# Diffusion steps with a PSUM operand in every VectorE instruction, and an init without GpSimd

## The chip, the cores and the metric

One core of a Trainium2 chip runs the whole program. Its engines are TensorE (PE; its weight loads are listed as PEld), VectorE (DVE), ScalarE (ACT), GpSimd (POOL) and SyncE (SP), which issues the DMAs. The metric is the device time in microseconds; the time before is the median of three runs.

## The reference

Four layers follow each other on an image of 48 x 48 pixels with 768 channels, all in fp32: attention with an MLP, a Fourier layer, a diffusion scan, and another Fourier layer. The change concerns the third:

```python
B_proj = silu(x @ W_B + b_B + B_bias).reshape(Bb, Hh, Ww, N, R)      # N = 64, R = 4
C_proj = silu(x @ W_C + b_C + C_bias).reshape(Bb, Hh, Ww, N, R)
Xb = silu(x @ W_X + b_X); alpha = sigmoid(x @ W_dec + b_dec)
theta = x @ W_th + b_th;  gamma = sigmoid(x @ W_lam + b_lam)
for i in range(NITERS):                                             # 12
    inj = _rope(B_base, theta * (i + 1)) * Xb
    Hst = diffuse(Hst)              # depthwise 3x3 convolution + conv_b
    if prev is None:
        Hst = alpha * Hst + inj
    else:
        Hst = alpha * Hst + (1.0 - gamma) * alpha * prev + gamma * inj
    prev = inj
Hg = _rope(C_base, theta * NITERS) * Hst
return silu(Ho @ W_out + b_out)     # Ho is Hg with its axes moved
```

## The kernel before, in words

The program runs attention, projection, MLP, first Fourier layer (`afno_first`), the scan (`scan_phase`) and the second Fourier layer one after the other. A tile framework inserts the semaphores and orders each engine's instructions.

In the scan a partition holds one column position of one of two image rows: rows of a pair sit at partitions 0 to 47 and 64 to 111, and 24 pairs (NPR) lie along the free axis. 256 channels (64 n times 4 r) make 6144 elements per partition.

The init (lines 722 to 835) forms everything that the steps need. Its weights `w` are loaded at line 729, when the scan begins. A loop `q` of six rounds takes four pairs (R4) each. For each pair 12 matmuls (line 758) make two PSUM tiles, `pa` and `pb`, four buffers each, and VectorE adds the bias on the way to `za` and `zb` (lines 759 and 760). ScalarE applies silu and sigmoid, and sine and cosine after a range reduction on VectorE (`reduce_angle`). Then VectorE and GpSimd share the elementwise work: `turn` (lines 793 to 798) rotates with two of its four products on GpSimd; GpSimd also multiplies by x (line 801) and by gamma (lines 820 and 825). The results are the state `H`, two sources `s0` and `s1`, `al` (alpha), `c1` (2 cos theta), and `cr`, which goes to DRAM for the end (line 835).

The source of each iteration follows a recurrence: with s for this iteration and s' for the last, the next is c1 * s - s'. It is written over s'.

The steps (lines 863 to 891) are 11 iterations over 8 groups of 8 channels n. TensorE does the convolution as a product with banded matrices (`bands`, line 872): 32 matmuls a group, 64 records[...]. Row 48 of the bands holds the convolution's bias, and row 48 of H holds ones. Since the init computes on all 128 partitions, it fills the gap rows 48 to 63 with other values; four DMAs (line 858, source `gap`) then set them in H, s0, s1 and c1. `alr` is alpha repeated over r, made by ScalarE (line 859). A group's PSUM tile (one of four, two banks each) is used so:

```python
V.tensor_tensor(y, ps[:, :, :half], alr[:, ch], ALU.mult)     # line 875
V.tensor_tensor(Hd, y, fl(sc), ALU.add)                       # line 878
GP.tensor_tensor(t, sc[:, ch], c1[:, m0 : m0 + GC], ALU.mult) # line 881
e = GP if gr % 8 in (1, 4, 7) else V
e.tensor_tensor(sn[:, ch], t, sn[:, ch], ALU.subtract)        # line 883
```

(shapes shortened). In the last iteration the source is not updated; `cr` is loaded (line 887) and H is multiplied by it into `hg`, six products a group (line 891). Then 24 pairs are transposed and multiplied by the output weights (lines 908 to 920).

Of the kernel before, what the change touches and what calls it, by code (L numbers as in the profile page):

```python
# [18 lines left out]
P = 128  # L19
# [655 lines left out]
def reduce_angle(nc, pool, th, n, name):  # L675

    MAGIC = 1.5 * 2.0**23
    C1 = 6.28125
    C2 = math.floor((2.0 * math.pi - C1) * 2.0**22) / 2.0**22
    C3 = 2.0 * math.pi - C1 - C2  # L680
    k = pool.tile([P, n], F32, tag="sc_k", name=f"{name}_k")
    r = pool.tile([P, n], F32, tag="sc_r", name=f"{name}_r")
    nc.vector.tensor_scalar(k, th, 1.0 / (2.0 * math.pi), MAGIC, ALU.mult, ALU.add)
    nc.vector.tensor_scalar(k, k, MAGIC, None, ALU.subtract)
    nc.vector.scalar_tensor_tensor(out=r, in0=k, scalar=-C1, in1=th, op0=ALU.mult, op1=ALU.add)
    nc.vector.scalar_tensor_tensor(out=r, in0=k, scalar=-C2, in1=r, op0=ALU.mult, op1=ALU.add)
    nc.vector.scalar_tensor_tensor(out=r, in0=k, scalar=-C3, in1=r, op0=ALU.mult, op1=ALU.add)
    PI = 3.1415925
    nc.vector.tensor_scalar(r, r, -PI, PI, ALU.max, ALU.min)
    a = pool.tile([P, n], F32, tag="sc_a", name=f"{name}_a")  # L690
    nc.scalar.activation(a, r, AF.Abs)
    return r, a


def scan_phase(tc, ident, wts, xT, xT_close, cr_d, out_open):
# [11 lines left out]
    (w_d, b0_d, b1_d, cb_d, bands_d, gap_d, wo_d, bo_d) = wts  # L707
    R4 = 4
    NQ = G // 2 // R4
    NPR = G // 2  # L710
    NCR = NN * RR
# [3 lines left out]
    with tc.tile_pool(name="sc_s", bufs=1, side="left") as sp:  # L715
        s0 = sp.tile([P, NN, RR, NPR], F32, tag="s0", name="s0")
        s1 = sp.tile([P, NN, RR, NPR], F32, tag="s1", name="s1")
        with tc.tile_pool(name="sc_state", bufs=1, side="left") as stp:
            H = stp.tile([P, NN, RR, NPR + 2], F32, tag="H", name="H")
            al = stp.tile([P, NN, NPR], F32, tag="al", name="al")  # L720
            c1 = stp.tile([P, NM, NPR], F32, tag="c1", name="c1")
            GP.memset(H, 0.0)
            with (
# [4 lines left out]
                w = wp.tile([P, NC, NA + NB2], F32, tag="w", name="w")  # L728
                nc.sync.dma_start(w, w_d.rearrange("(c p) n -> p c n", p=P))
                bias = load_bcast(nc, wp, b0_d, NA + NB2, "bias")  # L730
                bias1 = load_bcast(nc, tp, b1_d, NA + NB2, "zb")
# [5 lines left out]
                def temp(shape, tag, q, bufs=1):  # L737
                    return tp.tile([P, *shape], F32, tag=tag, name=f"{tag}_{q}", bufs=bufs)

                def sincos(th, q, nm):  # L740
                    r, a = reduce_angle(nc, tp, th, NM * R4, f"{nm}_{q}")
# [3 lines left out]
                    nc.scalar.activation(co.rearrange("p m t -> p (m t)"), a, AF.Sin, bias=halfpi, scale=-1.0)  # L745
                    return co, sn

                for q in range(NQ):
                    prs = slice(q * R4, (q + 1) * R4)
                    za = temp([NA, R4], "za", q)  # L750
                    zb = temp([NB2, R4], "zb", q)
                    for t in range(R4):
# [3 lines left out]
                        for ps, c0, n in ((pa, 0, NA), (pb, NA, NB2)):  # L756
                            for cc in range(NC):
                                nc.tensor.matmul(ps[:, :n], lhsT=xT[:, cc, tok : tok + P], rhs=w[:, cc, c0 : c0 + n], start=cc == 0, stop=cc == NC - 1)
                        V.tensor_tensor(za[:, :, t], pa[:, :NA], bias[:, :NA], ALU.add)
                        V.tensor_tensor(zb[:, :, t], pb[:, :NB2], bias[:, NA:], ALU.add)  # L760
# [7 lines left out]
                    alq = al[:, :, prs]  # L768
# [8 lines left out]
                    c1q = c1[:, :, prs]  # L777
                    V.tensor_scalar(c1q, cs, 2.0, None, ALU.mult)

                    def over_r(v, n):  # L780
                        return v.unsqueeze(2).to_broadcast([P, n, RR, R4])
# [5 lines left out]
                    def turn(out, in_, co, si, nm):  # L787
# [5 lines left out]
                        GP.tensor_tensor(m0, b, si, ALU.mult)  # L793
                        V.tensor_tensor(oa, a, co, ALU.mult)
                        V.tensor_tensor(oa, oa, m0, ALU.subtract)
                        GP.tensor_tensor(m1, b, co, ALU.mult)
# [4 lines left out]
                    GP.tensor_tensor(g.rearrange("p (n r) t -> p n (r t)", r=RR), g.rearrange("p (n r) t -> p n (r t)", r=RR), x.rearrange("p r t -> p (r t)").unsqueeze(1).to_broadcast([P, NN, RR * R4]), ALU.mult)  # L801
                    i03 = H[:, :, :, 1 + q * R4 : 1 + (q + 1) * R4]
# [6 lines left out]
                    V.tensor_tensor(be, alq, om.to_broadcast([P, NN, R4]), ALU.mult)  # L809
                    bc = temp([NN, R4], "bc", q)  # L810
                    gc = temp([NM, R4], "gc", q)
                    V.tensor_tensor(gc, c1q, ga.to_broadcast([P, NM, R4]), ALU.mult)
# [3 lines left out]
                    gab = ga.to_broadcast([P, NCR, R4])  # L816
                    flat = lambda v: v.rearrange("p n r t -> p (n r) t")

                    u = temp([NCR, R4], "u", q)
                    GP.tensor_tensor(u, i0, gab, ALU.mult)  # L820
                    t0 = s0[:, :, :, prs]
                    V.tensor_tensor(t0, g3, over_r(be, NN), ALU.mult)
                    V.tensor_tensor(flat(t0), flat(t0), u, ALU.add)
                    u = temp([NCR, R4], "u", f"{q}_1")
                    GP.tensor_tensor(u, g, gab, ALU.mult)
                    t1 = s1[:, :, :, prs]
# [4 lines left out]
                    V.tensor_tensor(ac, alq, cb.unsqueeze(2).to_broadcast([P, NN, R4]), ALU.mult)  # L831
                    V.tensor_tensor(i03, i03, over_r(ac, NN), ALU.add)
                    cr = temp([NCR, R4], "u", f"{q}_2")
                    turn(cr, c, cs12, sn12, "c")
                    nc.sync.dma_start(cr_d[:, q], cr)
            xT_close()
            K = 112
            GC = 8
            with (
# [11 lines left out]
                for gr in range(NN // GC):  # L851
                    ch = slice(gr * GC, (gr + 1) * GC)
                    nc.sync.dma_start(bands[:K, ch], bands_d[:, ch])
                    if gr == 0:
                        gap = slice(G, HD)
                        for t, n, v in ((c1, NM * NPR, 1), (s1, NCR * NPR, 0), (s0, NCR * NPR, 0), (H, NCR * (NPR + 2), 0)):
                            t = t[gap].rearrange("p n t -> p (n t)") if t is c1 else t[gap].rearrange("p n r t -> p (n r t)")
                            nc.sync.dma_start(t, gap_d[v : v + 1, :n].to_broadcast([HD - G, n]))
                    nc.scalar.copy(alr[:, ch], al[:, ch].unsqueeze(2).to_broadcast([P, GC, RR, NPR]))
                s = [s0, s1]  # L860
                for it in range(1, ITERS):
                    sc, sn = s[it % 2], s[(it + 1) % 2]
                    for gr in range(NN // GC):
                        ch = slice(gr * GC, (gr + 1) * GC)
                        m0 = (gr * GC) % NM
                        nm = f"{it}_{gr}"
                        ps = pss[gr % 4]
                        for k in range(GC):
                            n = gr * GC + k
                            cols = slice(k % 4 * RR * NPR, (k % 4 + 1) * RR * NPR)  # L870
                            for i, (r0, d) in enumerate(((0, 1), (HD, 1), (0, 0), (HD, 2))):
                                nc.tensor.matmul(ps[r0 : r0 + G, k // 4, cols], lhsT=bands[:K, n, i, :], rhs=H[:K, n, :, d : d + NPR], start=i < 2, stop=i >= 2)  # L872
                        half = GC * RR * NPR // 2
                        y = tp.tile([P, GC * RR, NPR], F32, tag="y", name=f"y_{nm}")
                        V.tensor_tensor(y.rearrange("p (b n) t -> p b (n t)", b=2), ps[:, :, :half], alr[:, ch].rearrange("p (b n) r t -> p b (n r t)", b=2), ALU.mult)  # L875
                        fl = lambda v: v[:, ch].rearrange("p n r t -> p (n r) t")
                        Hd = fl(H)[:, :, 1 : 1 + NPR]
                        V.tensor_tensor(Hd, y, fl(sc), ALU.add)  # L878
                        if it + 1 < ITERS:
                            t = tp.tile([P, GC, RR, NPR], F32, tag="t", name=f"t_{nm}")  # L880
                            GP.tensor_tensor(t, sc[:, ch], c1[:, m0 : m0 + GC].unsqueeze(2).to_broadcast([P, GC, RR, NPR]), ALU.mult)  # L881
                            e = GP if gr % 8 in (1, 4, 7) else V
                            e.tensor_tensor(sn[:, ch], t, sn[:, ch], ALU.subtract)  # L883
                        else:

                            cr = tp.tile([P, NQ, GC * RR, R4], F32, tag="cr", name=f"cr_{gr}", bufs=2)
                            nc.sync.dma_start(cr, cr_d[:, :, gr * GC * RR : (gr + 1) * GC * RR])
                            hg = sn.rearrange("p n r t -> p (n r t)").rearrange("p (t n) -> p n t", t=NPR)
                            for q in range(NQ):
                                prs = slice(q * R4, (q + 1) * R4)  # L890
                                V.tensor_tensor(hg[:, gr * GC * RR : (gr + 1) * GC * RR, prs], Hd[:, :, prs], cr[:, q], ALU.mult)
# [3 lines left out]
        with (  # L895
# [8 lines left out]
            for p2 in range(NPR // 2):  # L904
                ps = pt.tile([P, 512], F32, tag="t", name=f"ht_{p2}")
                for t in range(2):
                    for j in range(2):
                        nc.tensor.transpose(ps[:, (2 * t + j) * P : (2 * t + j + 1) * P], hg[:, 2 * p2 + t, j * P : (j + 1) * P], ident)
# [16 lines left out]
def block_kernel(ctx: ExitStack, tc: tile.TileContext, a: dict):  # L925
# [31 lines left out]
    x2T, x2T_close = opened("x2T", [P, NC, G * HD], "right")  # L957
    afno_first(tc, ident, a, xA, x2T)
# [9 lines left out]
    wts = [a[k] for k in ("W_scan", "b_scan", "bias_scan", "conv_b", "bands", "gap", "W_out", "b_out")]  # L968
    cr_d = dram.tile([P, 6, NN * RR, 4], F32, tag="cr_d", name="cr_d")
    x3 = scan_phase(tc, ident, wts, x2T, x2T_close, cr_d, out_open)  # L970
# [80 lines left out]
def shape_constants():  # L1051
# [18 lines left out]
    for h in range(2):  # L1070
# [9 lines left out]
        "gap": f(np.stack([np.full(NN * RR * 26, 1.0), np.full(NN * RR * 26, 2.0)]), 2, NN * RR * 26),  # L1080

# [10 lines left out]
def banded(w, b):  # L1092
# [6 lines left out]
    m = np.zeros((112, NN, 4, G), np.float32)  # L1099
    for i, dhs in enumerate(((1, 2), (None, 0), (0, 1), (2, None))):  # L1100
# [6 lines left out]
        if i < 2:  # L1107
            m[G, :, i, :] = b[:, None]
# [47 lines left out]
```

## Time and profile before

| | us |
|---|---|
| median of three runs (4768.79 to 4771.67) | 4770.26 |
| the profiled execution | 4773.5 |
| its span, first to last instruction | 4771.3 |
| first matmul of the scan's init starts | 3709.63 |
| its last add into H (line 832) starts | 3920.13 |
| first matmul of the steps starts | 3934.50 |
| first product of the steps (line 875) starts | 3952.45 |
| first matmul of the output product starts | 4283.39 |

The starts are on the axis of the profiled execution, counted from its first instruction. The page of the profile gives for each engine its busy time in forty slices, the groups of instructions by source line with mean duration and idle time before them, and the chain of work that ended last. Queries of the trace add the tables of busy time for chosen stretches, the durations of one line, the waits, and instructions in order of time. A busy VectorE instruction may include time in which it stands still: its duration runs from its start to its end, whatever held it up. In the group lines an entry such as `H<-y,s 128x768` names output and inputs with partitions and elements.

### The profile page before, as it was taken

To read this page: it belongs to the slowest core of one execution; us is meant where nothing else is said; L and a number is where in the kernel's file an instruction comes from. 1 tells how busy PE (TensorE), PEld (TensorE's weight loads), DVE (VectorE), ACT (ScalarE), POOL (GpSimd) and SP (SyncE) were. 2 spreads that over 40 slices of the span, in tenths; PEclk is the share of its full clock that TensorE was granted. 3 is DMA by queue.
4 is the path that set the end of the run, shared out by engine and by line. 5 is a ranking of instruction groups with operands and counts; after the bars stand their busy time and mean duration, and the time that the engine had idled before them with its cause. 6 is when DMAs were issued, how large, how long until landed. Compare 5 with 4: busy or idle time off the path is not lost.

```text
span 4771.3 us, 55325 instructions
## 1 busy us (share of the span) xinstructions
PE 4439.8 (93%) x23674; PEld 2736.8 (57%) x23674; DVE 1792.5 (38%) x2434; ACT 1045.8 (22%) x1660; POOL 449.8 (9%) x292
## 2 busy tenths in 40 slices
PE   8999699999999999989999999999998847789998
PEld 5555344444444444555555555556777637776776
DVE  4212155554555555410110100002343679983333
ACT  2111133333333333100110100002222330003221
POOL 0000000000000000110000000000000338630000
PEclk9999899999999999989999999999998978899887
DMA  4132522121212112151111111110000020010001
GB/s 153 40 84 64 127 41 50 30 50 40 50 30 50 30 33 54 43 133 50 50 50 50 50 53 48 49 47 2 3 5 1 31 65 18 2 31 6 18 20 30
DMA packets 144904, 212.46 MB, mean 45 GB/s; under 512 B 24620, under 2 KB 112684, under 8 KB 142236
## 3 DMA queue, kind: packets, MB, share of 16 engines
q1 hardware_dynamic: 144652, 208.85, 16.6%
q8 instruction: 188, 3.08, 0.3%
q14 instruction: 64, 0.52, 0.0%
HBM read 166.74 MB, written 42.07 MB: 44 GB/s over the span
## 4 chain that ended last, share of the span: by engine, by line
PE 82%; DVE 10%; ACT 2%; issue 2%; DMA 1%; SPq 1%; POOL 1%; DVEq 0%; POOLq 0%; ACTq 0%
PE s L342 18%; PE acc L528 12%; PE h L520 11%; PE av L363 9%; PE v L252 3%; DVE H L878 3%; PE pj L482 3%; PE q L167 3%; PE k L241 3%; PE f_f L996 2%; DVE y L875 2%; DVE s L883 2%; PE f_z L631 2%; PE f_z L630 1%; PE f_w L1040 1%
## 5 line engine op out<-in xcount | busy, mean ns | idle before, releaser
L342 PE MATMUL s<-qa,ka 128*128 128x384 f32 x2592 | 896.1, 496 | 41.0 <-DMA qa<-rh_d 40.0
L342 PEld LDWEIGHTS s<-qa,ka 128*128 128x128 f32 x2592 | 475.9, 190 | 457.1 <-issue 170.2
L352 DVE TENSOR_TENSOR acc<-acc,p 128x768 f32<-128x768 f32 x576 | 552.7, 959 | 487.8 <-ACT p L344 487.0
L344 ACT ACTIVATE p<-s 128x768 f32<-128x768 f32 x648 | 525.1, 811 | 820.2 <-PE s L342 820.2
L528 PE MATMUL acc<-w,ht 128*128 128x384 f32 x1728 | 581.6, 487 | 9.9 <-DMA w<-in_mlp_w_dram 9.9
L520 PE MATMUL h<-x2nT,w 128*128 128x384 f32 x1728 | 583.0, 488 | 5.6 <-ACT ln_sd L69 3.5
L528 PEld LDWEIGHTS acc<-w,ht 128*128 128x128 f32 x1728 | 329.3, 191 | 240.2 <-DMA w<-in_mlp_w_dram 10.5
L363 PE MATMUL av<-p,vt 128*64 128x384 f32 x2592 | 465.5, 494 | 0.0
L520 PEld LDWEIGHTS h<-x2nT,w 128*128 128x128 f32 x1728 | 329.3, 191 | 236.0 <-issue 6.3
L533 DVE TENSOR_TENSOR xA<-acc,xA 128x384 f32<-128x384 f32 x36 | 20.1, 557 | 1078.7 <-PE acc L528 1078.4
L872 PE MATMUL c<-H,bands 112*48 112x96 f32 x5632 | 266.8, 260 | 118.4 <-DVE y L875 67.8
L872 PEld LDWEIGHTS c<-H,bands 112*48 112x48 f32 x5632 | 257.8, 132 | 127.6 <-DVE y L875 75.8
L363 PEld LDWEIGHTS av<-p,vt 128*64 128x64 f32 x2592 | 166.9, 136 | 272.1 <-issue 272.1
L522 ACT ACTIVATE ht<-h,ml_b 128x384 f32<-128x384 f32 x144 | 83.6, 580 | 988.5 <-PE h L520 961.8
L477 POOL TENSOR_TENSOR pj_x<-pj_x,pj_b 128x768 f32<-128x768 f32 x18 | 34.3, 1913 | 2029.1 <-DVE acc L352 1874.7
L881 POOL TENSOR_TENSOR t<-s,c 128x768 f32<-128x768 f32 x80 | 168.1, 2106 | 65.0 <-DVE s L883 50.8
L241 PE MATMUL k<-xnT,w 128*128 128x384 f32 x432 | 148.9, 494 | 1.1 <-ACT rw L181 1.1
L252 PE MATMUL v<-w,xnT 128*128 128x384 f32 x432 | 149.0, 495 | 0.0
L878 DVE TENSOR_TENSOR H<-y,s 128x768 f32<-128x768 f32 x88 | 145.1, 1648 | 3.1
L631 PE MATMUL f_z<-f_w,f_o 97*96 97x96 f32 x800 | 142.3, 262 | 1.0 <-POOL f_o L620 1.0
L630 PE MATMUL f_z<-f_w,f_o 97*96 97x96 f32 x800 | 142.7, 262 | 0.0
L167 PE MATMUL q<-xnT,w 128*128 128x384 f32 x432 | 142.2, 488 | 0.0
(185 smaller groups left out, 4350.4 us busy)
## 6 DMA issues: line engine op xcount, KB each, us to landing
w<-in_mlp_w_dram SPq DMA_DIRECT2D x168, 384.0 KB
qa<-q_d SPq DMA_DIRECT2D x72, 288.0 KB
qa<-rw_d SPq DMA_DIRECT2D x72, 216.0 KB
x<-in_x_dram SPq DMA_DIRECT2D x18, 384.0 KB
w<-in_qkv_w_dram SPq DMA_DIRECT2D x18, 384.0 KB
q_d<-qT SPq DMA_DIRECT2D x6, 1152.0 KB
k_d<-kT SPq DMA_DIRECT2D x6, 1152.0 KB
v_d<-v SPq DMA_DIRECT2D x6, 1152.0 KB
```

What stands on the lines that cost most here:

```text
L167: nc.tensor.matmul(ps[:, :TB], lhsT=ws[0][:, cc, pr * P : (pr + 1) * P], rhs=xnT[:, cc, tok], start=cc == 0, stop=cc == NC - 1)
L241: nc.tensor.matmul(ps[:, :TB], lhsT=ws[1][:, cc, pr * P : (pr + 1) * P], rhs=xnT[:, cc, tok], start=cc == 0, stop=cc == NC - 1)
L252: nc.tensor.matmul(ps[:, :TB], lhsT=xnT[:, cc, (3 * blk + t) * P : (3 * blk + t + 1) * P], rhs=ws[2][:, cc, cols], start=cc == 0, stop=cc ...
L342: nc.tensor.matmul(ps[:, s, :QB], lhsT=kas[2 * (pr % 2) + s][:, kt * P : (kt + 1) * P], rhs=chunks[c][s][:, g, :], start=True, stop=True)
L344: nc.scalar.activation(p, ps[:, :, :QB], AF.Exp)
L352: nc.vector.tensor_tensor(probs[c], probs[c], p, ALU.add)
L363: nc.tensor.matmul(avs[c][rows, :QB], lhsT=pairs[pr][:, kt, rows], rhs=p[:, s, :], start=kt == 0, stop=kt == NT - 1)
L520: nc.tensor.matmul(ps[:, :TB], lhsT=w1s[f][:, cc, :], rhs=xnT[:, cc, :], start=cc == 0, stop=cc == NC - 1)
L528: nc.tensor.matmul(acc[t][i][:, :TB], lhsT=ht[:, t * P : (t + 1) * P], rhs=w2t[:, i * TB : (i + 1) * TB], start=k == 0, stop=k == NF - 1)
L631: nc.tensor.matmul(out, lhsT=o1[:, j, 0:2, :].rearrange("c r h -> c (r h)"), rhs=w2t[:, 1, :], start=False, stop=True)
L872: nc.tensor.matmul(ps[r0 : r0 + G, k // 4, cols], lhsT=bands[:K, n, i, :], rhs=H[:K, n, :, d : d + NPR], start=i < 2, stop=i >= 2)
L878: V.tensor_tensor(Hd, y, fl(sc), ALU.add)
```

## The change

Four things are altered in `scan_phase`, its helper and its caller.

The steps: the product with alpha is written back into PSUM, and the sum into H reads it from there. GpSimd still makes t; ScalarE copies t into the same PSUM tile, and VectorE's update reads it from PSUM. All updates are VectorE's. They stand one group later in the program (`after`), also the products with `cr`, of which there are now eight a group.

The ones row: it moves from row 48 to row 112 of H and bands. The init works on partitions 0 to 111 (`K`), so the gap DMAs and their input are removed; GpSimd sets partitions 96 to 127 before the init. Gap rows 48 to 63 keep what the init puts there, as the bands are zero in them.

The init: eight rounds of three pairs. GpSimd's products go to VectorE, except those with gamma, which ScalarE does as multiplications by a scalar per partition, three for each tile. `za` and `u` get two buffers, `cr` its own.

The weights: the caller opens `wsc` and loads it before `afno_first`.

```diff
-    R4 = 4
+    R4 = 3
+    K = 112
...
+            top = slice(96, P)
             GP.memset(H, 0.0)
+            for t, v in ((al, 0.0), (c1, 2.0), (s0, 1.0), (s1, 1.0), (H[:, :, :, 1 : 1 + NPR], 1.0)):
+                GP.memset(t[top], v)
...
-                w = wp.tile([P, NC, NA + NB2], F32, tag="w", name="w")
-                nc.sync.dma_start(w, w_d.rearrange("(c p) n -> p c n", p=P))
...
-                    za = temp([NA, R4], "za", q)
+                    za = temp([NA, R4], "za", q, 2)
...
-                                nc.tensor.matmul(ps[:, :n], lhsT=xT[:, cc, tok : tok + P], rhs=w[:, cc, c0 : c0 + n], start=cc == 0, stop=cc == NC - 1)
+                                nc.tensor.matmul(ps[:K, :n], lhsT=xT[:, cc, tok : tok + K], rhs=w[:, cc, c0 : c0 + n], start=cc == 0, stop=cc == NC - 1)
...
+                    def by_gamma(out, in_):
+                        for t in range(R4):
+                            nc.scalar.mul(out[:, :, t], in_[:, :, t], ga[:, 0, t : t + 1])
...
-                        GP.tensor_tensor(m0, b, si, ALU.mult)
+                        V.tensor_tensor(m0, b, si, ALU.mult)
...
-                        GP.tensor_tensor(m1, b, co, ALU.mult)
+                        V.tensor_tensor(m1, b, co, ALU.mult)
...
-                    GP.tensor_tensor(u, i0, gab, ALU.mult)
+                    by_gamma(u, i0)
...
-                    GP.tensor_tensor(u, g, gab, ALU.mult)
+                    by_gamma(u, g)
...
-                    cr = temp([NCR, R4], "u", f"{q}_2")
+                    cr = temp([NCR, R4], "cr", q)
                     turn(cr, c, cs12, sn12, "c")
-                    nc.sync.dma_start(cr_d[:, q], cr)
+                    nc.sync.dma_start(cr_d[:K, q], cr)
+            w_close()
             xT_close()
-            K = 112
+            K1 = K + 1
...
-                    nc.sync.dma_start(bands[:K, ch], bands_d[:, ch])
-                    if gr == 0:
-                        gap = slice(G, HD)
-                        for t, n, v in ((c1, NM * NPR, 1), (s1, NCR * NPR, 0), (s0, NCR * NPR, 0), (H, NCR * (NPR + 2), 0)):
-                            t = t[gap].rearrange("p n t -> p (n t)") if t is c1 else t[gap].rearrange("p n r t -> p (n r t)")
-                            nc.sync.dma_start(t, gap_d[v : v + 1, :n].to_broadcast([HD - G, n]))
+                    nc.sync.dma_start(bands[:K1, ch], bands_d[:, ch])
...
-                        V.tensor_tensor(y.rearrange("p (b n) t -> p b (n t)", b=2), ps[:, :, :half], alr[:, ch].rearrange("p (b n) r t -> p b (n r t)", b=2), ALU.mult)
...
-                        V.tensor_tensor(Hd, y, fl(sc), ALU.add)
...
-                            e = GP if gr % 8 in (1, 4, 7) else V
-                            e.tensor_tensor(sn[:, ch], t, sn[:, ch], ALU.subtract)
...
+                    pv = ps[:, :, :half]
+                    V.tensor_tensor(pv, pv, banks(alr, gr), ALU.mult)
+                    by_bank = lambda v: v.rearrange("p (b n) r t -> p b (n r) t", b=2)
+                    V.tensor_tensor(by_bank(H[:, ch])[:, :, :, 1 : 1 + NPR], pv.rearrange("p b (n t) -> p b n t", t=NPR), by_bank(sc[:, ch]), ALU.add)
+                    if it + 1 < ITERS:
+                        t = tp.tile([P, GC, RR, NPR], F32, tag="t", name=f"t_{it}_{gr}")
                         m0 = (gr * GC) % NM
...
+                        GP.tensor_tensor(t, sc[:, ch], c1[:, m0 : m0 + GC].unsqueeze(2).to_broadcast([P, GC, RR, NPR]), ALU.mult)
+                        nc.scalar.copy(pv, t.rearrange("p (b n) r t -> p b (n r t)", b=2))
...
+                def after(it, gr):
+
+                    sn = s[(it + 1) % 2]
+                    if it + 1 < ITERS:
+                        sb = banks(sn, gr)
+                        V.tensor_tensor(sb, pss[gr % 4][:, :, :half], sb, ALU.subtract)
+                        return
...
+                    for q in range(NQ):
+                        prs = slice(q * R4, (q + 1) * R4)
+                        V.tensor_tensor(hg[:K, nr, prs], Hd[:K, :, prs], crs[gr][:K, q], ALU.mult)
...
+                for i in range(len(steps) + 1):
+                    if i < len(steps):
+                        step(*steps[i])
+                    if i:
+                        after(*steps[i - 1])
...
     x2T, x2T_close = opened("x2T", [P, NC, G * HD], "right")
+    wsc, wsc_close = opened("wsc", [P, NC, a["W_scan"].shape[1]], "right")
+    nc.sync.dma_start(wsc, a["W_scan"].rearrange("(c p) n -> p c n", p=P))
     afno_first(tc, ident, a, xA, x2T)
...
-            m[G, :, i, :] = b[:, None]
+            m[112, :, i, :] = b[:, None]
```

## The prediction

> **What bounds the kernel now.** I read the busy table by stage first, then the groups of the diffusion steps, the tiles of one step, the waits, and the order of time of one group.
>
> The stages of the scan (stretch, length, busy time of each engine with its instruction count, granted TensorE clock, DMA share, GB/s):
>
> ```profile
> core 0: us, PE busy (x) PEld busy (x) DVE busy (x) ACT busy (x) POOL busy (x), PEclk, DMA share, GB/s
> 3700.00:3709.60 9.60, 0.86 (x6) 0.62 (x4) 1.17 (x3) 0.00 (x0) 5.64 (x1) 0.50 0.67 232
> 3709.60:3883.90 174.30, 157.78 (x576) 113.73 (x576) 128.62 (x205) 59.86 (x84) 57.65 (x34) 0.94 0.04 14
> 3883.90:3934.50 50.60, 0.04 (x1) 0.03 (x1) 36.25 (x54) 17.99 (x25) 20.06 (x10) 0.55 0.52 121
> 3934.50:3952.40 17.90, 13.31 (x256) 13.11 (x256) 11.08 (x5) 0.00 (x0) 17.90 (x10) 0.79 0.53 141
> 3952.40:4231.60 279.20, 216.07 (x4480) 207.73 (x4480) 272.22 (x186) 0.00 (x0) 202.17 (x99) 0.91 0.01 2
> 4231.60:4278.30 46.70, 39.16 (x903) 38.36 (x904) 45.61 (x85) 0.00 (x0) 1.84 (x1) 0.96 0.18 53
> ```
>
> VectorE is busy 272.22 of 279.20 us in the steps: it is the bound there, and ScalarE does nothing. In the 50.60 us before them TensorE stands still.
>
> Three lines on VectorE and GpSimd in the steps (duration min/median/max):
>
> ```profile
> L875 DVE TENSOR_TENSOR y<-c,alr x88: 940/945/955, 3952.4 to 4274.7; 128x768 f32<-128x768 f32 x88
> L878 DVE TENSOR_TENSOR H<-y,s x88: 957/1807/1919, 3953.4 to 4275.8; 128x768 f32<-128x768 f32 x88
> L883 DVE TENSOR_TENSOR s<-t,s x50: 957/2384/2587, 3932.9 to 4232.7; 128x768 f32<-128x768 f32 x50
> L881 POOL TENSOR_TENSOR t<-s,c x80: 1795/1820/2543, 3931.1 to 4227.5; 128x768 f32<-128x768 f32 x80
> ```
>
> All are 768 elements per partition. The one that reads PSUM and SBUF (y) never leaves 0.95 us; those that read SBUF twice need 0.96 us at best and 1.8 to 2.4 us usually. In order of time (start, length) the long ones end with a GpSimd instruction and not with their own work:
>
> ```profile
> 4053.42 0.94 DVE L875 TENSOR_TENSOR y<-c,alr 128x768 f32<-128x768 f32 x1
> 4053.58 1.82 POOL L881 TENSOR_TENSOR t<-s,c 128x768 f32<-128x768 f32 x1 [0.89 <-DVE s L883]
> 4054.40 1.81 DVE L878 TENSOR_TENSOR H<-y,s 128x768 f32<-128x768 f32 x1
> ```
>
> GpSimd ends at 4055.40; H ends 0.81 us later, at 4056.21: it stood still until then. The entry to the steps shows in the waits:
>
> ```profile
> PE pa L758 <- DMA w<-in_W_scan_dram: 8.8, 1, 8.8
> ...
>   DMA H<-in_gap_dram: 50.6, 1
> ```
>
> 8.8 us for the projection weights, and 50.6 us that end with the gap transfer into H, though most of them are VectorE's tail of the init: its last add into H (L832) starts at 3920.13.
>
> **What the Trainium skill says.** "SBUF — State Buffer", Who interferes with whom: VectorE with two SBUF inputs and a GpSimd instruction that reads SBUF exclude each other, and with at most one SBUF input they don't; a VectorE instruction in a 2-port mode is also excluded. The trace agrees: 0.945 us against 1.807, and the tensor_scalar of four elements (om, L807) takes 0.952 us beside GpSimd. "VectorE: DVE Perf Modes", The perf-mode tier table: an fp32 tensor_tensor runs at one element per cycle with SBUF or with a PSUM operand; 0.945 and 0.957 us agree. "TensorE: Matmul & The Clock Gate", What's actually happening: the array starts at half clock and activity releases it; here 17 step matmul records per us at clock 0.50, 30 at 1.00. "ScalarE: Activation LUTs", Step-by-step: ScalarE writes PSUM at lower latency than SBUF; no run here shows it, and I take no gain.
>
> **The change part by part.** All on the time axis of before's profile.
>
> *Weights loaded early.* The 7.3 us transfer moves behind the MLP's last weight load in SP's queue. It waits for the MLP's memory (its last VectorE add starts at 3243.9); behind it in the queue stand block 2's weights, issued only at 3299.7. So it is hidden, with 450 us of cover. TensorE starts the init at 3702.2, when VectorE has freed the previous phase, not at 3709.6. Without the idle it also stays warm: a token takes 6.2 us (3736.88 to 3743.08), against 8.7 for the first now. Bias loads no longer stand behind 1.8 MB.
>
> *Init in eight rounds of three tokens.* TensorE needs 3 x 6.2 = 18.6 us a round, so VectorE's chain decides. The last evacuation that the first round needs starts at 3702.2 + 12.4 + 3.1 = 3717.7. From it to the next round's, by the instruction order of the changed kernel as built:
> - ScalarE up to the sine: 0.7 to the first table load, then loads of 1.28 us. Silu of 768 takes 0.85 (between 1.06 for 1024 and 0.42 for 256). Rounds 2, 4 and 6 load three tables: sine ready at 7.5 us, but VectorE has work until 8.1. The others load five: 0.7 + 5 x 1.28 + 2 x 0.85 + sigmoids, abs and gaps of 1.3 = 10.1.
> - VectorE after it, each at its issue distance without GpSimd (512 elements 0.60 us, 1024 1.13, so 384 0.47 and 768 0.87): turn of the injection 6 x 0.47, small ones 1.55, four of 768 3.5, second turn 2.8, evacuations 0.5 + 0.6 + 0.6: 12.35.
>
> So rounds take 22.45 or 20.45 us, against 31.9 for four tokens now (za to za, 3766.36 to 3798.34), where GpSimd's wait alone is visible in bc (1.455 us for 128 elements) and u (2.848). Seven rounds: 4 x 22.45 + 3 x 20.45 = 151.15. The eighth until H is ready: 10.1, 1.0 for memsets of the PSUM buffers, 8 more = 19.1. H is ready at 3717.7 + 170.3 = 3888. GpSimd's six memsets (6656 elements took 5.64, so some 23 us from 3699) end near 3722, before the first write to H (3729); the u products on ScalarE (3 x 256 each, about 1.1 us) lie beside VectorE's additions. If that cover fails, a round grows by 1 to 2 us.
>
> *Gap transfers gone.* TensorE no longer waits from 3921.4 (end of L832) to 3934.5. Late next are the bands, 5.5 MB: they queue behind the seventh cr store, some 22 us before H is ready, and at the 280 GB/s of before's burst last 20 us; group 0 needs one eighth. Hidden. Row 112 in place of row 48 changes no tile size. The cr stores are eight instead of six, and their loads come in pieces of 384 in place of 512 bytes; three buffers instead of two cover them in the last iteration.
>
> *Entry.* TensorE is cold after its idle: group 0 is 64 records at 17 per us, 3.8 us. First step product at 3891.8; now it is at 3952.45.
>
> *Steps.* VectorE keeps 3 instructions a group (80 groups), now all PSUM with SBUF; GpSimd keeps one (1.82 us). The built order is product(i+1), update(i), sum(i+1). update(i) waits for ScalarE's new copy into PSUM, which waits for sum(i): 0.957 + 0.09 (VectorE to ScalarE, as in L689 to L691) + 0.825 (as alr, 128x768) + 0.03 back + 0.88 for the update = 2.78; product(i+1) lies under the copy. I add 0.05 for the sequencer's waits: 2.83 us. Behind the waiting update stand sum(i+1) and, through H, TensorE's next iteration, eight groups off. A copy into PSUM and a product from PSUM into PSUM are in no row here: below, if both overlap fully, VectorE's three at 0.88 give 2.64; above, 0.3 us more give 3.1. TensorE needs 64 / 30 = 2.13 us warm. Eighty groups: 226. Last iteration, 8 groups: 1.86 for product and sum (as at 4245 to 4251), 8 products of 96 elements at 0.22 (six of 128 take 1.56): 3.65 x 8 = 29.
>
> End of the steps: 3891.8 + 226 + 29 = 4147, now 4278.3: 131 us less. The profiled execution took 4773.5 us with a span of 4771.3; 4773.5 - 131 = 4642, and against the median of 4770.26 it is 4639. I forecast **4639 us**. What follows (output product, second AFNO) is untouched.
>
> **Rivals.**
> - TensorE becomes the bound: if the clock falls back to half and stays, a group is 64 / 17 = 3.76 us and 80 groups cost 75 more: 4714. For: 0.50 appears after gaps of few us (4055.9 to 4058.9). Against: with 2.13 of 2.83 us busy the gaps shrink, and at 4231 to 4269 it ran at 1.00 throughout. 6%.
> - The init gains little: if a round needs 25.5 us (four more than my mean of 21.6, the present pace per token being 8.0 us x 3 = 24), eight rounds cost 31 more: 4670. For: VectorE takes over five products a round, and ScalarE's tables are reloaded in eight rounds, not six. 13%.
> - Slower: GpSimd still excludes VectorE although one operand is in PSUM. Then sum and update take 1.9 and 1.95 us around the serial copy: 1.9 + 0.09 + 0.83 + 0.03 + 1.95 = 4.8 us, 80 groups cost 158 more: 4797. It decides from 2.83 + 131/80 = 4.5 us a group. Against: y, 945 ns whether GpSimd runs or not. 4%.
> - The same time, an accident between these: 1%.
>
> **How the numbers follow.** Main forecast 76%, own range 4615 to 4672: 2.64 us a group is 15 less, 3.1 is 22 more, one us a round is 8 either way. The range for 8 in 10 reaches past the init rival: 4612 to 4685. This kernel's measurement tells 0.2% (9.5 us) from no change. Faster 76 + 6 + 13 = 95%, same 1%, slower 4%.
>
> **What would show it.** Steps right: product, sum and update all at 0.93 to 0.98 us with GpSimd at 1.8; ScalarE's copy at about 0.8; a group every 2.8 us; first product near 3892. Wrong: sum or update above 1.5 us; ScalarE's copy above 1.1; TensorE's clock under 0.8 in the steps; rounds of 25 us; a wait on bands ahead of group 0.

## The result, and the profile after

The changed kernel takes 4811.35 us (median of four runs, 4808.41 to 4815.06), against 4770.97 us for the kernel before (four runs, 4768.79 to 4775.51): a ratio of 1.0084, with a 95% interval of 1.0066 to 1.0101. It is 40 us slower, where 131 us less were forecast. The profiled execution took 4813.98 us, with a span of 4812.2.

The steps' lines, to be held against the four shown of before (duration min/median/max in ns, first and last start in us):

```profile
L879 DVE TENSOR_TENSOR c<-c,alr x88: 955/957/1035, 3903.0 to 4313.9; 128x768 f32<-128x768 f32 x88
L881 DVE TENSOR_TENSOR H<-c,s x88: 947/949/972, 3904.0 to 4315.0; 128x768 f32<-128x768 f32 x88
L897 DVE TENSOR_TENSOR s<-c,s x80: 946/958/959, 3905.9 to 4293.1; 128x768 f32<-128x768 f32 x80
L885 POOL TENSOR_TENSOR t<-s,c x80: 1799/1827/2112, 3887.5 to 4284.8; 128x768 f32<-128x768 f32 x80
```

The operand split does all that was hoped of it: the sum has fallen from 1807 to 949 ns and the update from 2384 to 958, beside a GpSimd instruction that still takes 1827. And yet the first product starts at 3903.0 and the last at 4313.9, 411 us for what took 322 before. The waits of the same stretch say what for (who waits for whom: us in total, times, longest):

```profile
engine line waited for: us in total, times, longest us
...
PE c L877 <- DMA bands<-in_bands_dram: 188.3, 8, 37.1
DVE c L879 <- PE c L877: 176.9, 9, 24.7
```

Eight waits, one for each piece of the bands. In order of time (start, length, then idle time before it and its releaser):

```profile
3879.09 158.97 SPq L860 DMA_DIRECT2D bands<-in_bands_dram  x6
...
3897.88 5.12 PE L877 MATMUL c<-H,bands 113*48 113x96 f32 x64 [37.10 <-DMA bands<-in_bands_dram]
...
3924.44 5.36 PE L877 MATMUL c<-H,bands 113*48 113x96 f32 x64 [21.44 <-DMA bands<-in_bands_dram]
...
4084.49 5.84 PE L877 MATMUL c<-H,bands 113*48 113x96 f32 x70 [21.31 <-DMA bands<-in_bands_dram]
```

The state is ready at 3886.4 (the last add into H, line 837, starts at 3885.5 and takes 0.95). Group 0 starts at 3897.9, and each of the next seven groups 26.6 us after the last: a piece of 113 rows of 6144 bytes in 26.65 us is 26 GB/s. The stages (the columns are those of the table by stage in the prediction):

```profile
core 0: us, PE busy (x) PEld busy (x) DVE busy (x) ACT busy (x) POOL busy (x), PEclk, DMA share, GB/s
3700.00:3890.00 190.00, 158.82 (x614) 109.10 (x614) 152.22 (x372) 110.83 (x181) 25.77 (x8) 0.90 0.06 19
...
3950.00:4000.00 50.00, 9.82 (x128) 9.29 (x128) 5.38 (x6) 1.60 (x2) 3.60 (x2) 0.53 0.06 26
4000.00:4050.00 50.00, 9.77 (x128) 9.43 (x128) 5.38 (x6) 1.60 (x2) 3.60 (x2) 0.57 0.06 26
...
4100.00:4150.00 50.00, 50.00 (x1218) 50.00 (x1215) 48.67 (x56) 14.46 (x18) 33.06 (x19) 1.00 0.01 3
```

A DMA share of 0.06 is one sixteenth of the core's 16 DMA engines: it reads as one that works all the time and fifteen that do nothing. The packets in the trace agree: from 3900 to 4100 there is just one under way for 180 of the 200 us, and a row of 6144 bytes takes 0.238 us. Once the bands are in (last row), VectorE is busy 48.67 of 50 us and the steps run as fast as forecast. The first iteration takes 189.8 us from product to product, each later one 22.15.

Why one engine? The bands now fill 113 partitions in place of 112, and the load is one DMA of 113 rows. The Trainium skill, "DMA: Bandwidth & Descriptors", Why a DMA increments its semaphore by 16 and not by 1, states under "How many engines" that a transfer is spread over the largest number up to 16 that divides the rows of both sides, so 127 partitions get one engine. 113 is a prime, so by this rule its load gets one engine too, and 112 = 7 x 16 gets sixteen. The prediction did not use the rule; the first four experiments test it.

### The profile page after: what moved, and what is told of

Its sections match the earlier page's. It is cut to its first block, busy times and chain, and to the rows that moved or that the text cites. A ratio compares the mean times of both kernels' runs of the same rounds, so it can differ in the third digit from the quotient of the medians.

```text
span 4812.2 us, 55521 instructions
## 1 busy us (share of the span) xinstructions
PE 4432.7 (92%) x23674; PEld 2727.5 (57%) x23674; DVE 1694.9 (35%) x2588; ACT 1141.4 (24%) x1809; POOL 314.5 (7%) x225
## 5 line engine op out<-in xcount | busy, mean ns | idle before, releaser
L877 PE MATMUL c<-H,bands 113*48 113x96 f32 x5632 | 258.4, 256 | 188.3 <-DMA bands<-in_bands_dram 188.3
L533 DVE TENSOR_TENSOR xA<-acc,xA 128x384 f32<-128x384 f32 x36 | 20.1, 558 | 1076.7 <-PE acc L528 1076.4
L877 PEld LDWEIGHTS c<-H,bands 113*48 113x48 f32 x5632 | 250.8, 129 | 196.3 <-issue 125.5
L885 POOL TENSOR_TENSOR t<-s,c 128x768 f32<-128x768 f32 x80 | 146.6, 1833 | 411.1 <-ACT c L886 252.6
L879 DVE TENSOR_TENSOR c<-c,alr 128x768 f32<-128x768 f32 x88 | 84.7, 962 | 176.9 <-PE c L877 176.9
L886 ACT COPY c<-t 128x768 f32<-128x768 f32 x80 | 64.3, 803 | 341.1 <-DVE H L881 205.5
```

## The experiments

All ratios are to runs of the kernel before on the same chip (medians there 4774 to 4777 us). Differences in us between two experiments are between medians that may come from different chips. e3 and e4 have one run each.

| run | us | runs | ratio, 95% interval |
|---|---|---|---|
| e1_split | 4629.9 | 4 | 0.9689 [0.9673, 0.9706] |
| e2_rows128 | 4630.53 | 4 | 0.9697 [0.9681, 0.9713] |
| e3_rows118 | 4707.81 | 1 | |
| e4_before113 | 4922.53 | 1 | |
| e5_steps_back | 4722.14 | 2 | 0.9887 [0.9867, 0.9907] |
| e6_no_gpsimd | 4684.66 | 2 | 0.9808 [0.9789, 0.9828] |
| e7_w_late | 4631.76 | 4 | 0.9701 [0.9685, 0.9717] |
| e8_steps_only | 4689.94 | 2 | 0.9819 [0.9800, 0.9839] |
| e9_w_memory | 4640.6 | 4 | 0.9720 [0.9704, 0.9736] |
| e11_init_gp | 4676.02 | 4 | 0.9798 [0.9782, 0.9815] |

### The bands in two loads

```diff
-                    nc.sync.dma_start(bands[:K1, ch], bands_d[:, ch])
+                    nc.sync.dma_start(bands[:K, ch], bands_d[:K, ch])
+                    nc.sync.dma_start(bands[K:K1, ch], bands_d[K:K1, ch])
```

> The changed kernel with each bands load cut in two: rows 0 to 111, and row 112 by itself. Theory A (a transfer whose partition count is 113 is carried by one of the 16 DMA engines, 26 us for each of eight loads, and the first iteration of the steps goes at that pace): all bands are there by about 3890, the first product starts near 3892, groups keep the 2.66 us that the later iterations show, the steps end near 4132 instead of 4318: about 4625 us. Rival B (the loads are slow for another reason: they start late, the queue is held up, memory is busy): the groups of the first iteration still come 26 us apart, about 4811 us.

4629.9 us: 181 us less than the changed kernel, for a load cut into its first 112 rows and its last. The wait of TensorE is no longer for a DMA:

```profile
PE c L878 <- DVE H L837: 26.5, 1, 26.5
```

This is idle time of TensorE while VectorE finishes the init. By stage (columns as above):

```profile
3890.00:3910.00 20.00, 16.97 (x397) 16.29 (x394) 17.35 (x20) 5.17 (x7) 11.90 (x7) 1.00 0.79 188
3910.00:3930.00 20.00, 20.00 (x491) 20.00 (x488) 19.45 (x22) 5.62 (x7) 12.41 (x8) 1.00 0.01 4
```

The second half of the bands comes with a DMA share of 0.79, beside the steps, and is in by 3910. The steps' first iteration takes 24.2 us. The 181 us can be counted in the two traces: the first iteration is 189.8 - 24.2 = 165.6 shorter; from H ready to the first product it is 16.6 against 7.5, 9.1 shorter; and H is ready at 3880.0 against 3886.4, since the Fourier layer before the scan ended later in the other execution (last write of x2T at 3708.4 against 3702.5). The sum is 181. Some 175 of it belong to the load; the last 6 are a difference between two executions of a layer that the change does not touch.

### More rows: 128 and 118

Rows of zeros are added to the bands, in memory and in the load: 128 rows, and 118 = 2 x 59.

```diff
-                    nc.sync.dma_start(bands[:K1, ch], bands_d[:, ch])
+                    nc.sync.dma_start(bands[:128, ch], bands_d[:, ch])
...
-    m = np.zeros((113, NN, 4, G), np.float32)
+    m = np.zeros((128, NN, 4, G), np.float32)
```

> The changed kernel with the bands padded by zero rows to 128 partitions, one load for each group, matmuls on 113 rows as before. A: 128 rows spread over 16 engines, about 4625 us although 13% more bytes are moved. B: as slow as now or slower, 4811 to 4840 us.

> The changed kernel with bands of 118 partitions (2 x 59). If the number of engines is the largest divisor of the partition count up to 16, two engines carry a load: 13.6 us each, the eighth is there near 3868.6 + 109 = 3978 instead of 4084, so about 106 us less: 4705 us. If every count that is no multiple of 16 falls to one engine: 27 us each, about 4820 us.

128 rows are 13% more bytes than 113, and the kernel is 181 us faster: 4630.53, the same as the split. 118 rows come to 4707.81, within 3 us of what two engines give. Its stage with the bands on the way:

```profile
3900.00:3950.00 50.00, 16.09 (x192) 15.16 (x192) 9.88 (x11) 3.21 (x4) 7.20 (x4) 0.55 0.13 54
```

0.13 is two sixteenths, and 54 GB/s is twice the 26. In the packets of its trace two are under way for 86 of the 95 us from 3885 to 3980; while the bands load in e1 (112 rows) and e2 (128 rows) it is sixteen for the largest part. So neither the bytes nor "more than 112" decide, but the divisor; the page's rule holds at all four sizes tried (112, 113, 118, 128).

### The kernel before with 113 rows

Nothing of the change but the extra row, all zeros:

```diff
-                    nc.sync.dma_start(bands[:K, ch], bands_d[:, ch])
+                    nc.sync.dma_start(bands[: K + 1, ch], bands_d[:, ch])
...
-    m = np.zeros((112, NN, 4, G), np.float32)
+    m = np.zeros((113, NN, 4, G), np.float32)
```

> The kernel before with one zero row more in the bands, loaded but not used: nothing else of the change. A: each load takes 26 us on one engine, and the gap transfers stand behind the first loads on it; the eighth load is there near 4100 and group 7 of the first iteration starts there instead of near 3962: about 138 us more, 4900 to 4915 us. B (the slowness belongs to something else in the change): 4771 us.

4922.53, some 145 us slower than before: the row alone does the harm. TensorE's long wait there does not name the bands:

```profile
PE c L872 <- DMA H<-in_gap_dram: 157.0, 1, 157.0
```

The gap transfers stand behind loads of the bands and come late with them. A reader who took this line at its word would repair the wrong transfer.

### The steps alone, and all but the steps

e8_steps_only is the kernel before with the new steps (product into PSUM, sum from PSUM, ScalarE's copy, VectorE's update one group later). e5_steps_back is e1_split with the old steps, whose core is

```diff
-                    V.tensor_tensor(pv, pv, banks(alr, gr), ALU.mult)
+                    y = tp.tile([P, GC * RR, NPR], F32, tag="y", name=f"y_{it}_{gr}")
+                    V.tensor_tensor(y.rearrange("p (b n) t -> p b (n t)", b=2), pv, banks(alr, gr), ALU.mult)
...
-                        nc.scalar.copy(pv, t.rearrange("p (b n) r t -> p b (n r t)", b=2))
+                        sn = s[(it + 1) % 2]
+                        e = GP if gr % 8 in (1, 4, 7) else V
+                        e.tensor_tensor(sn[:, ch], t, sn[:, ch], ALU.subtract)
```

> The kernel before with the new steps alone (product written back into PSUM, sum from PSUM, ScalarE's copy of t, updates on VectorE from PSUM, one group later); init in six rounds, gap transfers, weights and 112 rows of bands as before. Theory: the steps gain 80 x 1.33 = 106 us whatever stands before them: 4777 - 106 = 4671, and groups of 2.66 us. Then the rest of the change is worth 147 - 106 = 41 us. Rival (the steps' gain depends on the new init, say through the clock that TensorE has at the entry): 4700 or more.

> As e1_split (bands in two loads, 4630 us), but the steps' VectorE and GpSimd instructions as in the kernel before: product into SBUF, sum from SBUF, update of groups 1, 4 and 7 on GpSimd, no copy by ScalarE. The init and the ones row stay new. Theory (the PSUM operands are worth what the forecast says): a group goes from 2.66 us back to before's pace (80 groups in 319 us, 3.99 each, with the sum at 1.8 us in the median), 80 x 1.33 = 106 us more: 4736, and the sum and update lines show 1.8 to 2.4 us. Rival (most of e1's gain is from the init and the ones row, and the steps gain little): 4630 to 4660.

e8 gains 87 us (4776.8 - 4689.94), e5 55 (4776.8 - 4722.14), together 142; both at once, in e1, gain 147. So the parts add up. In e5 the old durations are back:

```profile
L883 DVE TENSOR_TENSOR H<-y,s x88: 945/1807/2603, 3884.8 to 4223.3; 128x768 f32<-128x768 f32 x88
L890 DVE TENSOR_TENSOR s<-t,s x50: 957/2380/2605, 3882.3 to 4181.0; 128x768 f32<-128x768 f32 x50
```

Both expectations of 106 us were too high, because I had taken the two paces from unequal stretches. Counted alike, from the first product to that of the last iteration, 80 groups take 298.8 us before, 223.6 in e1 and 221.9 in e8: 75 to 77 us. The rest of e8's 87 lies at the entry: before, VectorE makes five updates ahead of its first product, which starts 17.95 us after the first matmul (3934.50 to 3952.45); in e8 it is 5.2 us (3941.6 to 3946.8). The same five updates explain most of what looks like a loss in e5: its first iteration takes 52.4 us from product to product and before's 32.7, but e5 makes none of them ahead of the first product. From H ready to the first product of the second iteration, e5 takes 58.5 us and before 63.7.

### No GpSimd in the steps

As e5, with VectorE also making t and all updates:

```diff
-                        GP.tensor_tensor(t, sc[:, ch], c1[:, m0 : m0 + GC].unsqueeze(2).to_broadcast([P, GC, RR, NPR]), ALU.mult)
+                        V.tensor_tensor(t, sc[:, ch], c1[:, m0 : m0 + GC].unsqueeze(2).to_broadcast([P, GC, RR, NPR]), ALU.mult)
...
-                        e = GP if gr % 8 in (1, 4, 7) else V
+                        e = V
```

> As e5_steps_back, but VectorE also makes t and all the updates, so GpSimd is idle in the steps; all of VectorE's operand pairs but the product's are SBUF with SBUF. VectorE has four instructions a group in place of 2.6 to 3. Theory (exclusion by GpSimd is what makes SBUF pairs slow): each takes 0.96 us or less, issued 0.88 apart, 4 x 0.88 = 3.5 us a group, 80 x 0.85 = 68 more than e1_split: 4698, that is faster than e5 although VectorE does more. Rival (two SBUF operands are slow in themselves, 1.8 us, GpSimd or not): three at 1.8 and one at 0.95, 6.3 us a group: 4920.

4684.66, 37 us faster than e5 although VectorE has four instructions a group and an engine less helps it. All three with two SBUF operands now take their 0.94 us every time:

```profile
L883 DVE TENSOR_TENSOR H<-y,s x88: 939/945/952, 3890.3 to 4187.6; 128x768 f32<-128x768 f32 x88
L887 DVE TENSOR_TENSOR t<-s,c x80: 941/943/950, 3889.5 to 4163.7; 128x768 f32<-128x768 f32 x80
L890 DVE TENSOR_TENSOR s<-t,s x80: 942/946/951, 3891.2 to 4165.4; 128x768 f32<-128x768 f32 x80
```

An iteration is 27.77 us, 3.47 a group: four instructions issued 0.87 apart. So it was GpSimd's work at the same time, and not the operands' place by itself, that made them slow, as the Trainium skill, "SBUF — State Buffer", Who interferes with whom, has it. With one operand in PSUM (e1) GpSimd's help is free, and another 55 us come.

### The weights

e7_w_late moves the load of w behind the Fourier layer in the program; e9_w_memory also gives w its old place in the scan's own memory.

```diff
-    wsc, wsc_close = opened("wsc", [P, NC, a["W_scan"].shape[1]], "right")
-    nc.sync.dma_start(wsc, a["W_scan"].rearrange("(c p) n -> p c n", p=P))
...
+                w = wp.tile([P, NC, NA + NB2], F32, tag="w", name="w")
+                nc.sync.dma_start(w, w_d.rearrange("(c p) n -> p c n", p=P))
```

> As e1_split, but the projection weights are loaded after the first Fourier layer, as in the kernel before. Theory (the early load takes 8 us off the front of the init): TensorE waits some 8 us for w before its first matmul of the init, H is ready some 8 us later, 4638. Rival (something else holds the init's first round, as GpSimd's memsets or the tables on ScalarE, and the wait is absorbed): 4630, the same as e1_split.

> As e1_split, but the weights w have their place in the scan's own memory again, as in the kernel before, and not a tile of their own (in e7_w_late they kept that tile, SyncE issued the load at 3244.0 us all the same, and the edit so moved nothing). Theory (it is the place of its own that takes 8 us off): w can land only when the Fourier layer has left that memory, TensorE waits some 8 us for it, starts cold, and H is ready 8 to 10 us later: 4639. Rival (the wait is absorbed by the tables or GpSimd's memsets): 4630.

e7 was a blank: 4631.76, as e1. SyncE, which has nothing to wait for before it, issued the load at 3244.0 all the same. What delays the load is its memory, and e9 brings the wait back:

```profile
PE pa L762 <- DMA w<-in_W_scan_dram: 8.8, 1, 8.8
```

It takes 4640.6, 10.7 us more than e1; the intervals of the two ratios just touch. In the traces, each counted from the end of its Fourier layer, the first matmul of the init and H are later by 7.5 and 7.7 us (first matmul 3715.3 against 3703.2, last add into H 3891.3 against 3879.0, with the last 64-partition write of x2T at 3706.5 against 3701.9). This part was worth 8 us at the front of the init, and none of it was absorbed. In e9's profiled execution the first iteration is also 5.2 us longer than e1's (29.4 against 24.2) and the entry 2.0 shorter; what makes that first iteration longer stays open.

### GpSimd's products in the init

e1_split with before's five products a round on GpSimd again:

```diff
-                        V.tensor_tensor(m0, b, si, ALU.mult)
+                        GP.tensor_tensor(m0, b, si, ALU.mult)
...
-                        V.tensor_tensor(m1, b, co, ALU.mult)
+                        GP.tensor_tensor(m1, b, co, ALU.mult)
...
-                    by_gamma(u, i0)
+                    GP.tensor_tensor(u, i0, ga.to_broadcast([K, NCR, R4]), ALU.mult)
...
-                    by_gamma(u, g)
+                    GP.tensor_tensor(u, g, ga.to_broadcast([K, NCR, R4]), ALU.mult)
```

and the product of g with x in the same way.

> As e1_split, but in the init the five products a round that had been GpSimd's in the kernel before are GpSimd's again (two in each turn, the one with x, the two with gamma); still eight rounds of three pairs, weights early, no gap transfers, new steps. Theory (GpSimd's products and the exclusion are what made the init slow): rounds of 24 us, before's 8.0 us a pair times 3, in place of some 20.5: 8 x 3.5 = 28 more, 4658. Rival (the smaller rounds and the additional buffers made the gain): 4630 to 4638.

4676.02, 46 us more, where 28 were expected: a round takes 25.3 us from add to add into H (3746.1 to 3923.4 in seven), in e1 20.1. VectorE gets rid of products and comes out slower: it is busy 22.7 us a round against 18.3, and idle 2.6 against 1.9. Even its small instructions now stand still (groups by shape: busy us, mean ns of one, idle before):

```profile
L821 DVE TENSOR_TENSOR bc<-be,gc 112x96 f32<-112x96 f32 x14 | 16.9, 1245 | 0.0
L777 DVE TENSOR_SCALAR th<-th 112x96 f32<-112x96 f32 x8 | 11.3, 1410 | 0.0
```

In e1 the same two take 250 and 203 ns:

```profile
L821 DVE TENSOR_TENSOR bc<-be,gc 112x96 f32<-112x96 f32 x16 | 3.4, 250 | 0.0
L777 DVE TENSOR_SCALAR th<-th 112x96 f32<-112x96 f32 x8 | 1.6, 203 | 0.0
```

In the round around 3842 us of e11, the two bc instructions take 1.52 and 0.97 us and end 0.1 us after two GpSimd instructions do.

e1_split and e2_rows128 are also the versions that beat both kernels: about 3% under the kernel before, and as fast as each other.

## Why the prediction was wrong

The step that failed stands under *Gap transfers gone*: the bands "at the 280 GB/s of before's burst last 20 us; group 0 needs one eighth. Hidden. Row 112 in place of row 48 changes no tile size." The tile's size did not change; the number of rows that a DMA writes did, from 112 to 113, and with it the number of engines that carry the load, from 16 to 1. I carried a rate over from a transfer of another shape. The bands took 8 x 26.6 us in place of 20, and no cover of 22 us can hide that. Taking the fault out of the changed kernel gives back some 175 us (e1); putting it alone into the kernel before costs 145 (e4). None of the rivals had a DMA in it. The slower one was about GpSimd's exclusion, which the lines of 949 and 958 ns beside GpSimd refute; the prediction's list of signs did name "a wait on bands ahead of group 0".

The rest of the sum is seen in e1_split, which is the forecast kernel with this one fault taken out: 4629.9 us against 4639, or 147 us less than before on its own chip, against 131. Term by term, on e1's trace:

- *Weights loaded early*: right, 8 us (e9).
- *Init in eight rounds*: H ready at 3880, forecast 3888. Seven rounds took 140.9 us, not 151.15. VectorE's part was right: from the sine to the next round's last evacuation of pa 12.4 to 12.7 us, forecast 12.35. ScalarE's part was too long: from that evacuation to the sine it took 8.6 or 5.8 us (10.6 in the first round), not 10.1 or 8.1. From the second round on the round's first table load lies ahead of the evacuation, so that silu begins as soon as it ends (load at 3778.44, evacuation until 3783.87, silu at 3783.90). The u products on ScalarE were under-sized (three take 1.7 and 2.1 us, at 650 and 786 ns each, not 1.1), but the cover held: VectorE waited 3.7 us for them in all eight rounds.
- *Entry*: first product 7.5 us after H, forecast 3.8. In order of time:

```profile
3881.01 6.15 POOL L886 TENSOR_TENSOR t<-s,c 128x768 f32<-128x768 f32 x3 [157.47 <-DVE s L833]
3881.22 2.17 DVE L802 TENSOR_TENSOR m_c<-zb,t12c 112x384 f32<-112x384 f32 x1
3883.31 2.17 DVE L803 TENSOR_TENSOR cr<-zb,t12s 112x384 f32<-112x384 f32 x1
3885.51 2.06 DVE L804 TENSOR_TENSOR cr<-cr,m_c 112x384 f32<-112x384 f32 x1
3887.50 0.95 DVE L880 TENSOR_TENSOR c<-c,alr 128x768 f32<-128x768 f32 x1
```

The last round's turn of cr still stands in VectorE's queue ahead of the first product, with two SBUF operands, just when GpSimd begins its first three t. Its three instructions of 0.55 us take 2.1 each, 4.75 us more together: the very exclusion that the change was to remove. But without it TensorE would have set the time. In e9 GpSimd starts its t after the first product, the turn's instructions take 0.55 us, and the product still starts 5.6 us after H, since it waits for group 0:

```profile
3897.80 0.97 DVE L881 TENSOR_TENSOR c<-c,alr 128x768 f32<-128x768 f32 x1 [2.71 <-PE c L879]
```

So of the 3.7 us that the forecast lacks, some 2 are the exclusion's and the rest TensorE's.

- *TensorE's pace*: misread. The 17 and 30 records per us are what a window of 1 us shows, but such a window also counts the records that reach over its ends. Twenty us of before at clock 1.00 (4245 to 4265) hold 492 records, under 25 per us, and group follows group by 2.64 us wherever TensorE runs without a wait, as in e2; group 0 at clock 0.50 takes 5.1 us there, not 3.8, and the first rival's group at half clock would be about as long, not 3.76. No harm came of it in the steps, but that was luck: the forecast counted on 0.7 us of room between TensorE and the chain (2.13 against 2.83), and there is 0.13 (2.64 against 2.77).
- *Bands on all engines*: not wholly hidden either. In e1 the last four pieces are issued behind the eighth cr store, from 3888.0 on, when H is already there, and the first iteration takes 24.2 us; in e2 all eight are issued by 3858.6, and it takes 22.2.
- *Steps*: 2.77 us a group in the settled iterations (22.15 / 8), forecast 2.83; 80 groups 223.6, forecast 226. The order product, update, sum and the wait for ScalarE's copy hold: the copy into PSUM takes 0.803 us and the product from PSUM into PSUM 0.956, so both unknown costs were small. The last iteration's groups take 3.1, forecast 3.65.

Summed for the init, the entry, the steps and the last iteration, -8 + 3.7 - 2.4 - 4 makes 11 us less than the forecast; the profiled executions (4632.03 and 4773.5) differ by 141.5, 10.5 more than the 131. So the other terms were right in the main, with errors of both signs that come to 11 us together, and one edit costed at nothing was worth more than all of them.

## What to carry to other kernels

Where a change alters the number of partitions that a DMA reads or writes, even by one row, look at the divisors of the new number before using any rate measured with the old one; a DMA share of one sixteenth in the stage is the sign, and a second small DMA for the odd row, or padding, is the cure. An edit costed at nothing deserves the same question as the others: what shape has the thing that is supposed to hide it. And to free VectorE of GpSimd it can be enough to keep one operand in PSUM; sharing elementwise work between the two on SBUF operands was slower here than leaving GpSimd out (e6 against e5; in the init e1 against e11, where ScalarE took the two products with gamma).

## What the runs showed of the hardware that was not expected

- One DMA engine of the sixteen moved 26 GB/s here (113 rows), two moved 54 (118 rows).
- The fp32 copy of 128x768 from SBUF into PSUM by ScalarE took 0.803 us (0.83 for the copy alr<-al into SBUF), and VectorE's product from PSUM back into PSUM 0.956, against 0.945 into SBUF.
- ScalarE's multiplication by a scalar per partition took 650 and 786 ns for 256 elements that are written three apart; the slower one reads H, where they lie 26 apart, the other za, where they lie three apart.
- Beside GpSimd, an instruction of VectorE with 96 elements took 1.245 us in the mean (alone 0.25). In the round looked at it ended with GpSimd's instruction: what it loses goes by the length of that one and not by its own.
